# A two-layer graph network on 128 graphs: transposes of A and of score rows taken from TensorE to VectorE block transposes and GpSimd-issued DMAs

## The chip, the cores and the metric

The kernel runs on one core of a Trainium2 chip. Its engines work side by side, each through its own queue in order: TensorE (PE in the profile, with its weight loads as PEld) multiplies and can transpose; VectorE (DVE) and ScalarE (ACT) do the work element by element; GpSimd (POOL) and SyncE (SP) issue DMAs. Products land in PSUM, everything else lies in SBUF or in DRAM. The metric is the device time of one execution in microseconds (us); less is better.

## The reference

128 graphs of 128 nodes with 512 features; `adj` is a weighted 128x128 matrix for each. Cut to what matters (B = 128 graphs):

```python
# layer 0: graph attention, then K = 3 powers of the transition matrix
h = maximum(layernorm(x), 0)
Xw = h @ Wv + bv
sj, si = Xw @ aw[:512, 0], Xw @ aw[512:, 0]
e = leaky_relu(sj[:, None, :] + si[:, :, None] + ab[0], 0.2)     # score rows: sj runs along the row
alpha = adj * exp(e)
transition = alpha / (sum(alpha, -1, keepdims=True) + 1e-12)
H, Xk = 0, h
for k in range(3):
    H = H + Xk @ Wk[k] + bk[k]
    Xk = transition @ Xk
x = x + relu(H)
# layer 1
h2 = maximum(layernorm(x), 0)
q, k = split(h2 @ Wqk);  v = h2 @ Wv1
agg = adj @ (k * mask)
w = mask / sqrt(512) * sum(q * agg, -1)
x = x + softmax(w, axis=nodes)[:, :, None] * v
```

All data is fp32, and `mask` is given as an input.

## The kernel before

The kernel takes the graphs in pairs (G = 2, NP = 64 pairs) and is unrolled. Two algebraic turns matter for what follows. sj and si need no 512x512 product: two sums of h with fixed vectors u (`score_sums`) give them. And q times agg is h2 (Wq Wk^T) against A h2, so layer 1 multiplies h2 by two 512x512 matrices (`strassen1`) and A by h2 (`aggregate`). Both layers do their large products by a Strassen scheme with seven products P1 to P7, in the order 1, 6, 7, 5, 2, 3, 4. The framework puts the instructions of each engine in an order of its own, from the data they need and a model of their times, with the program's order as priority; it also sets the waits. A tile from a pool with `bufs=n` has n buffers in turn; a new tile waits until the oldest is no longer read.

Rows that have to be seen by all partitions are made by TensorE: `spread` transposes a column that is broadcast along the free axis.

```python
    def spread(dst, col):
        nc.tensor.transpose(dst, col.to_broadcast([P, P]), ident)
    # [...]
    def score_sums(p):
        h = H[p]
        s = S[p] = small.tile([P, G, 2], FP, name="s")
        for j in range(G):
            for a in range(2):
                junk = front.tile([P, D], FP, name="junk", bufs=1)
                nc.vector.scalar_tensor_tensor(junk, h[:, j, :], 1.0, u_bc[:, a, :], op0=OP.mult,
                                               op1=OP.mult, accum_out=s[:, j, a:a + 1])

    def by_blocks(h):
        hd = dram.tile([G, P, D], FP, name="hd")
        nc.sync.dma_start(hd.rearrange("g n d -> n g d"), h)
        hv = front.tile([P, G, Q, P], FP, name="hv")
        v = hd.rearrange("g (q b) (c i) -> c b (g q) i", b=S32, i=P)
        for c in range(DC):
            nc.sync.dma_start(hv[c * S32:(c + 1) * S32].rearrange("p g q i -> p (g q) i"), v[c])
        return hv

    def transposed(hv, dst):
        for j in range(G):
            nc.vector.transpose(dst[:, j].rearrange("p f (n b) -> p f n b", n=Q),
                                hv[:, j].rearrange("p n (f a) -> p f n a", f=Q))

    def attention(p):
        a, s = ag.pop(p), S.pop(p)
        pz = ps_t.tile([P, DC, P], FP, name="pt")
        for j in range(G):
            spread(pz[:, j, :], s[:, j, 0:1])
        z = front.tile([P, G, N], FP, name="z", bufs=1)
        for j in range(G):
            nc.vector.tensor_scalar(z[:, j, :], pz[:, j, :], s[:, j, 1:2], cz, op0=OP.add, op1=OP.add)
        nc.vector.scalar_tensor_tensor(z, z, 0.2, z, op0=OP.mult, op1=OP.max)
        ex = front.tile([P, G, N], FP, name="ex")
        nc.scalar.activation(ex, z, AF.Exp)
        d = small.tile([P, 2, G], FP, name="d")
        for j in range(G):
            nc.vector.scalar_tensor_tensor(ex[:, j, :], ex[:, j, :], 1.0, a[:, j, :], op0=OP.mult,
                                           op1=OP.mult, accum_out=d[:, 0, j:j + 1])
        nc.vector.tensor_scalar(d[:, 0], d[:, 0], 1e-12, None, op0=OP.add)
        nc.vector.reciprocal(d[:, 1], d[:, 0])
        t = T[p] = front.tile([P, G, N], FP, name="t")
        for j in range(G):
            nc.vector.tensor_scalar(t[:, j, :], ex[:, j, :], d[:, 1, j:j + 1], None, op0=OP.mult)
        pa = ps_t.tile([P, DC, P], FP, name="pt")
        for j in range(G):
            nc.tensor.transpose(pa[:, j, :], a[:, j, :], ident)
        AT[p] = front.tile([P, G, N], FP, name="aT", bufs=3)
        for j in range(G):
            b = p * G + j
            nc.scalar.activation(AT[p][:, j, :], pa[:, j, :], AF.Copy, scale=maskT[:, b:b + 1])

    def t_transposed(p):
        t, tt = T.pop(p), front.tile([P, G, 2, N], FP, name="tt")
        pt = ps_t.tile([P, DC, P], FP, name="pt")
        for j in range(G):
            nc.tensor.transpose(pt[:, j, :], t[:, j, :], ident)
        nc.scalar.copy(tt[:, :, 0, :], pt[:, :G, :])
        pt = ps_t.tile([P, DC, P], FP, name="pt")
        for j in range(G):
            nc.tensor.matmul(pt[:, j, :], t[:, j, :], tt[:, j, 0, :], start=True, stop=True)
        nc.scalar.copy(tt[:, :, 1, :], pt[:, :G, :])
        TT[p] = tt
```

`by_blocks` and `transposed` are a transpose without TensorE, and were there before: h goes to DRAM, is read back with its 32-row blocks exchanged, and VectorE transposes each 32x32 block. `ex` in `attention` is exp(e) times adj, `t` the transition matrix, and `AT` is A^T with the mask, from a transpose by TensorE.

```python
    def strassen0(p, steps):
        # [...]
        product(ba, 1, True)
        nc.vector.tensor_add(s[:, 0], a, hi)
        nc.vector.tensor_add(s[:, 1], a, lo)
        product(bb, 6, True)
        nc.vector.tensor_add(s[:, 2], b, s[:, 1])
        steps[0]()
        product(bc, 7, True)
        product(bb, 5, False)
        nc.vector.tensor_add(s[:, 3], b, s[:, 0])
        nc.vector.tensor_add(hb[:, 1, HD:], c, s[:, 3])
        steps[1]()
        product(ba, 2, False)
        nc.vector.tensor_add(hb[:, 0, :HD], a, lo)
        product(bb, 3, False)
        nc.vector.tensor_add(hb[:, 0, HD:], b, s[:, 0])
        product(bc, 4, False)
        nc.vector.tensor_add(hb[:, 1, :HD], c, s[:, 2])
        # [...]

    def strassen1(p):
        # [...]
        product(a, 1, True)
        nc.scalar.copy(s[:, 0], a)
        product(b, 6, True)
        nc.vector.tensor_add(s[:, 1], b, s[:, 0])
        product(c, 7, True)
        product(b, 5, False)
        nc.vector.tensor_add(s[:, 2], b, s[:, 0])
        nc.vector.tensor_add(o[1][1], c, s[:, 2])
        product(a, 2, False)
        nc.scalar.copy(o[0][0], a)
        product(b, 3, False)
        nc.vector.tensor_add(o[0][1], b, s[:, 0])
        product(c, 4, False)
        nc.vector.tensor_add(o[1][0], c, s[:, 1])
        return yv

    def aggregate(p, yv):
        h2, at = H2.pop(p), AT.pop(p)
        w = small.tile([P, 6, G], FP, name="w")
        for j in range(G):
            pa = ps_t.tile([P, D], FP, name="pt")
            nc.tensor.matmul(pa, at[:, j, :], h2[:, j, :], start=True, stop=True)
            junk = front.tile([P, D], FP, name="junk", bufs=1)
            b = p * G + j
            nc.vector.scalar_tensor_tensor(
                junk.rearrange("p (k d) -> p k d", k=2), pa.rearrange("p (k d) -> p k d", k=2),
                wscale[:, b:b + 1], yv[:, j, :, 0, :], op0=OP.mult, op1=OP.mult,
                accum_out=w[:, 0, j:j + 1])
        return w

    def finish(p, yv, w):
        pw = ps_t.tile([P, DC, P], FP, name="pt")
        for j in range(G):
            spread(pw[:, j, :], w[:, 0, j:j + 1])
        nc.vector.tensor_reduce(w[:, 1], pw[:, :G, :], AX.X, OP.max, negate=True)
        # [... exp of both rows with their sums, the weight of each node, x1 += weight * v ...]
        nc.sync.dma_start(out[p * G:(p + 1) * G].rearrange("b n d -> n b d"), x1)
```

The loop over pairs. In turn p, layer 0 of pair p runs with the attention of pair p + 1 between its products, then layer 1 of pair p - 1; `finish` (the softmax over the nodes) of an earlier pair runs inside the next layer 0.

```python
    for p in range(NP + 1):
        if p < NP:
            if p + 1 < NP:
                n = p + 1
                steps = (lambda: (begin(n), attention(n), end()), lambda: t_transposed(n))
            else:
                steps = (end, lambda: None)
            strassen0(p, steps)
            if p + 1 < NP:
                propagate(p + 1)
        # [...]
        if p < NP:
            H2[p] = norm_relu(X1[p], "h2", late["p"])
            hv2 = by_blocks(H2[p])
        if p > 0:
            yv = strassen1(p - 1)
            w = aggregate(p - 1, yv)
        if p + 1 < NP:
            prepare0(p + 1)
        if p > 0:
            ends.append((p - 1, yv, w))
        if p < NP:
            X2[p] = late["p"].tile([P, G, 2, HC, N], FP, name="x2")
            transposed(hv2, X2[p].rearrange("p j h c n -> p j (h c) n"))
            a = {(j, kh): X2[p][:, j, kh:kh + 1].rearrange("p k c n -> p k (c n)")
                 for j in range(G) for kh in range(2)}
            SX2[p] = left_sums(a, late["p"], "sx2", [1, HD])
        if p + 2 < NP:
            norm0(p + 2)
            score_sums(p + 2)
    end()
```

`late["p"]` is a pool with one buffer for each tile: h2, X2 and yv are single.

Of the kernel before, what the change touches and what calls it, by code (L numbers as in the profile page):

```python
# [8 lines left out]
FP = mybir.dt.float32  # L9
# [6 lines left out]
def kernel(  # L16
# [220 lines left out]

    H, HV, S, X, SX, AT, T, TT, X1, H2, X2, SX2 = ({} for _ in range(12))

# [7 lines left out]
    def score_sums(p):  # L248

        h = H[p]  # L250
        s = S[p] = small.tile([P, G, 2], FP, name="s")
        for j in range(G):
            for a in range(2):
                junk = front.tile([P, D], FP, name="junk", bufs=1)
                nc.vector.scalar_tensor_tensor(junk, h[:, j, :], 1.0, u_bc[:, a, :], op0=OP.mult,  # L255
                                               op1=OP.mult, accum_out=s[:, j, a:a + 1])

# [15 lines left out]

    def attention(p):

        a, s = ag.pop(p), S.pop(p)
        pz = ps_t.tile([P, DC, P], FP, name="pt")
        for j in range(G):
            spread(pz[:, j, :], s[:, j, 0:1])
        z = front.tile([P, G, N], FP, name="z", bufs=1)  # L280
        for j in range(G):
            nc.vector.tensor_scalar(z[:, j, :], pz[:, j, :], s[:, j, 1:2], cz, op0=OP.add, op1=OP.add)
        nc.vector.scalar_tensor_tensor(z, z, 0.2, z, op0=OP.mult, op1=OP.max)
        ex = front.tile([P, G, N], FP, name="ex")
        nc.scalar.activation(ex, z, AF.Exp)
        d = small.tile([P, 2, G], FP, name="d")
        for j in range(G):
            nc.vector.scalar_tensor_tensor(ex[:, j, :], ex[:, j, :], 1.0, a[:, j, :], op0=OP.mult,
                                           op1=OP.mult, accum_out=d[:, 0, j:j + 1])
        nc.vector.tensor_scalar(d[:, 0], d[:, 0], 1e-12, None, op0=OP.add)  # L290
        nc.vector.reciprocal(d[:, 1], d[:, 0])
        t = T[p] = front.tile([P, G, N], FP, name="t")
        for j in range(G):
            nc.vector.tensor_scalar(t[:, j, :], ex[:, j, :], d[:, 1, j:j + 1], None, op0=OP.mult)

        pa = ps_t.tile([P, DC, P], FP, name="pt")
        for j in range(G):
            nc.tensor.transpose(pa[:, j, :], a[:, j, :], ident)  # L298
        AT[p] = front.tile([P, G, N], FP, name="aT", bufs=3)
        for j in range(G):  # L300
            b = p * G + j
            nc.scalar.activation(AT[p][:, j, :], pa[:, j, :], AF.Copy, scale=maskT[:, b:b + 1])

    def t_transposed(p):

        t, tt = T.pop(p), front.tile([P, G, 2, N], FP, name="tt")
        pt = ps_t.tile([P, DC, P], FP, name="pt")
        for j in range(G):
            nc.tensor.transpose(pt[:, j, :], t[:, j, :], ident)  # L309
# [46 lines left out]
    def strassen0(p, steps):  # L356
# [53 lines left out]

    def aggregate(p, yv):

        h2, at = H2.pop(p), AT.pop(p)
        w = small.tile([P, 6, G], FP, name="w")
        for j in range(G):
            pa = ps_t.tile([P, D], FP, name="pt")
            nc.tensor.matmul(pa, at[:, j, :], h2[:, j, :], start=True, stop=True)  # L417
            junk = front.tile([P, D], FP, name="junk", bufs=1)
            b = p * G + j
            nc.vector.scalar_tensor_tensor(  # L420
                junk.rearrange("p (k d) -> p k d", k=2), pa.rearrange("p (k d) -> p k d", k=2),
                wscale[:, b:b + 1], yv[:, j, :, 0, :], op0=OP.mult, op1=OP.mult,
                accum_out=w[:, 0, j:j + 1])
        return w

    def finish(p, yv, w):

        pw = ps_t.tile([P, DC, P], FP, name="pt")
        for j in range(G):
            spread(pw[:, j, :], w[:, 0, j:j + 1])  # L430
        nc.vector.tensor_reduce(w[:, 1], pw[:, :G, :], AX.X, OP.max, negate=True)
        for j in range(G):
            ej = front.tile([P, N], FP, name="ej")
            nc.scalar.activation(ej, pw[:, j, :], AF.Exp, bias=w[:, 1, j:j + 1],
                                 accum_out=w[:, 2, j:j + 1])
        nc.vector.tensor_add(w[:, 3], w[:, 0], w[:, 1])
        nc.scalar.activation(w[:, 4], w[:, 3], AF.Exp)
# [100 lines left out]
```

## Time and profile before

| what | value |
|---|---|
| time, median of 3 runs | 2418.58 us (2418.56 to 2419.78) |
| span of the profiled execution | 2418.3 us |
| TensorE busy | 2378.8 us, 98% |
| VectorE busy | 1786.8 us, 74% |
| ScalarE busy | 650.5 us, 27% |
| GpSimd busy | 0.7 us |
| DMA queue of SyncE | 232624 packets, 216.65 MB, 30.5% of the 16 DMA engines' span |
| mean granted TensorE clock | 0.998 |

A line of a group reads: source line, engine, operation, output<-inputs, shapes, how often | busy us in total, mean ns of one | us that the engine sat idle just before them <- what ended it. In a timeline the two numbers ahead are the start and the length in us. A fp32 matmul shows as two instructions, a fp32 transpose as one. Matmuls follow each other in a pipeline, so that the distance of their starts is shorter than the length of one. A line of waits reads: engine and its work <- what it waited for: us in total, how often, longest.

### The profile page before, as it was taken

Reading aid. Unit: us, or ns where it says so; the run is one execution under the profiler, and the core shown is the slowest. Engines: PE = TensorE matmul, PEld = TensorE weight load, DVE = VectorE, ACT = ScalarE, POOL = GpSimd, SP = SyncE. Lnnn points to the kernel's source line nnn. Section 1 sums busy time; section 2 is a strip of 40 time slices with the busy share of each in tenths; the row PEclk is TensorE's granted clock in tenths of the full one; section 3 lists DMA queues with packets and bytes.
Section 4 is the critical chain, followed back from the end, with each engine's and each line's share of the span. In section 5 each row is a group of like instructions: output and inputs, shape, how many; then the busy total and the mean of one; then the engine's idle time right before and its main releaser. Section 6 shows DMA issues by size and latency. Waiting matters only on the chain.

```text
span 2418.3 us, 27245 instructions
## 1 busy us (share of the span) xinstructions
PE 2378.8 (98%) x9289; PEld 1694.5 (70%) x9289; DVE 1786.8 (74%) x4768; ACT 650.5 (27%) x1557; POOL 0.7 (0%) x6
## 2 busy tenths in 40 slices
PE   6999999999999999999999999999999999999997
PEld 4777677677676676776776776776766767767764
DVE  6777777777777777777777777777777777777764
ACT  3222222222222222223222222222222222232221
POOL 0000000000000000000000000000000000000000
PEclk9999999999999999999999999999999999999999
DMA  7233233233133233232332332332332332323311
GB/s 219 82 84 101 81 92 101 66 106 101 64 109 93 71 101 95 77 101 88 85 101 81 92 100 65 108 100 64 108 93 72 101 95 78 100 87 86 97 52 52
DMA packets 236986, 220.48 MB, mean 91 GB/s; under 512 B 14384, under 2 KB 170160, under 8 KB 236848
## 3 DMA queue, kind: packets, MB, share of 16 engines
q1 hardware_dynamic: 232624, 216.65, 30.5%
q10 hardware_dynamic: 4224, 2.10, 0.3%
q8 instruction: 73, 1.20, 0.2%
q14 instruction: 65, 0.53, 0.1%
HBM read 118.03 MB, written 100.66 MB: 90 GB/s over the span
## 4 chain that ended last, share of the span: by engine, by line
PE 96%; DVE 2%; DMA 1%; issue 0%; ACT 0%; SPq 0%; DVEq 0%; ACTq 0%
PE pm L346 79%; PE pt L325 9%; PE pt L417 4%; PE pt L97 1%; PE pt L313 1%; PE pt L298 1%; PE pt L309 1%; DMA bk_bc<-in_L_gnn_bk_dram 0%; DMA hd<-h 0%; DVE st L220 0%; DMA hv<-hd 0%; DMA w<-in_L_gnn_Wqk_dram 0%; DMA xg<-in_x_dram 0%; DVE x L271 0%; PE pm L208 0%
## 5 line engine op out<-in xcount | busy, mean ns | idle before, releaser
L346 PE MATMUL pm<-t,sx 128*128 128x256 f32 x2304 | 518.6, 380 | 1.4 <-DVE sx L333 1.4
L346 PEld LDWEIGHTS pm<-t,sx 128*128 128x128 f32 x2304 | 433.4, 190 | 57.4 <-DVE sx L333 2.0
L346 PE MATMUL pm<-b,x 128*128 128x256 f32 x1536 | 363.0, 380 | 0.0
L346 PE MATMUL pm<-f,sx 128*128 128x512 f32 x768 | 344.8, 598 | 0.3
L346 PEld LDWEIGHTS pm<-b,x 128*128 128x128 f32 x1536 | 282.6, 191 | 59.3 <-issue 29.6
L327 ACT COPY x<-pt 128x512 f32<-128x512 f32 x256 | 148.7, 581 | 500.6 <-PE pt L325 500.6
L346 PEld LDWEIGHTS pm<-f,sx 128*128 128x128 f32 x768 | 141.6, 191 | 193.7 <-issue 154.4
L346 PE MATMUL pm<-e,x 128*128 128x512 f32 x512 | 242.5, 596 | 6.5 <-DVE x L271 6.5
L325 PE MATMUL pt<-tt,h 128*128 128x256 f32 x1024 | 231.5, 379 | 0.0
L325 PEld LDWEIGHTS pt<-tt,h 128*128 128x128 f32 x1024 | 194.9, 190 | 26.2
L255 DVE SCALAR_TENSOR_TENSOR junk<-h,u_bc 128x512 f32<-128x512 f32 x256 | 176.4, 689 | 7.8 <-ACT h L235 0.9
L346 PE MATMUL pm<-b,sx 128*128 128x256 f32 x768 | 176.5, 379 | 0.0
L346 PE MATMUL pm<-t,x 128*128 128x256 f32 x768 | 176.2, 379 | 0.0
L235 ACT ACTIVATE h<-x,rs 128x512 f32<-128x512 f32 x128 | 97.2, 806 | 289.9 <-PE pt L417 277.1
L271 DVE STREAM_TRANSPOSE x<-hv 128x512 f32<-128x512 f32 x256 | 166.4, 688 | 6.6 <-DMA hv<-hd 5.7
L346 PEld LDWEIGHTS pm<-e,x 128*128 128x128 f32 x512 | 97.8, 191 | 102.8 <-issue 92.3
L346 PEld LDWEIGHTS pm<-t,x 128*128 128x128 f32 x768 | 146.2, 190 | 19.6
L346 PEld LDWEIGHTS pm<-b,sx 128*128 128x128 f32 x768 | 146.0, 190 | 19.5
L406 DVE TENSOR_TENSOR yv<-pm,s 128x512 f32<-128x512 f32 x64 | 44.3, 692 | 128.5 <-PE pm L346 128.5
L235 ACT ACTIVATE h<-xg,rs 128x512 f32<-128x512 f32 x128 | 97.2, 806 | 119.8 <-DVE rs L232 119.8
L417 PE MATMUL pt<-h,aT 128*128 128x512 f32 x256 | 120.5, 593 | 0.5 <-ACT h L235 0.5
L346 PE MATMUL pm<-e,sx 128*128 128x512 f32 x256 | 120.3, 592 | 0.0
(101 smaller groups left out, 2511.3 us busy)
## 6 DMA issues: line engine op xcount, KB each, us to landing
hd<-h SPq DMA_DIRECT2D x128, 512.0 KB, 3.1
hv<-hd SPq DMA_DIRECT2D x512, 128.0 KB, 3.3
xg<-in_x_dram SPq DMA_DIRECT2D x64, 512.0 KB, 3.6
out_dram<-x SPq DMA_DIRECT2D x64, 512.0 KB, 3.1
ag<-in_adj_dram SPq DMA_DIRECT2D x64, 128.0 KB, 3.0
w<-in_L_gnn_Wqk_dram ACTq DMA_DIRECT2D x8, 256.0 KB, 5.0
b<-in_L_gnn_Wk_dram SPq DMA_DIRECT2D x8, 256.0 KB, 3.4
wv_sb<-in_L_gnn_Wv_dram SPq DMA_DIRECT2D x4, 256.0 KB, 5.3
```

Source lines behind the costliest of these rows:

```text
L97: nc.tensor.transpose(dst, col.to_broadcast([P, P]), ident)
L235: nc.scalar.activation(h[:, j, :], src[:, j, :], AF.Relu, bias=rs[:, 1, j:j + 1], scale=rs[:, 0, j:j + 1])
L255: nc.vector.scalar_tensor_tensor(junk, h[:, j, :], 1.0, u_bc[:, a, :], op0=OP.mult, op1=OP.mult, accum_out=s[:, j, a:a + 1])
L271: nc.vector.transpose(dst[:, j].rearrange("p f (n b) -> p f n b", n=Q), hv[:, j].rearrange("p n (f a) -> p f n a", f=Q))
L298: nc.tensor.transpose(pa[:, j, :], a[:, j, :], ident)
L309: nc.tensor.transpose(pt[:, j, :], t[:, j, :], ident)
L313: nc.tensor.matmul(pt[:, j, :], t[:, j, :], tt[:, j, 0, :], start=True, stop=True)
L325: nc.tensor.matmul(pt[:, c].rearrange("p k n -> p (k n)"), h[:, j, at:at + P], tt[:, j].rearrange("p k n -> p (k n)"), start=True, stop=True)
L327: nc.scalar.copy(X[p][:, 1:3, j, kh].rearrange("p k c n -> p c k n"), pt)
L346: nc.tensor.matmul(bank[:, :r.shape[-1]], left[i][:, k, c * P:(c + 1) * P], r, start=(first and at == 0), stop=(at == len(chunks) - 1), sk ...
L406: nc.vector.tensor_add(o[0][1], b, s[:, 0])
L417: nc.tensor.matmul(pa, at[:, j, :], h2[:, j, :], start=True, stop=True)
```

## The change

Four things are done together.

1. A^T: A is loaded a second time by GpSimd's DMAs, with its 32x32 blocks exchanged, and one block transpose on VectorE then gives A^T. The two TensorE transposes of each pair and their PSUM tile go.
2. Score rows: the column sums are written to a 128x32 tile (cleared once), VectorE transposes its blocks, GpSimd writes the rows to DRAM with two DMAs and reads them back with one DMA broadcast to all partitions (`spread_pair`). It is used for layer 0's rows (pz) and for the rows of layer 1's softmax (pw); the first pair's pz and the last pair's pw still go by TensorE.
3. A h2 is computed between the products of layer 1 (after P7 and after P2) in place of after P4, and held in PSUM until P4 is through. The layer norm and the score sums of pair p + 2 are moved ahead, the sums to after P5.
4. z takes no tile of its own but the room of `s[:, 1]`, which is free once the sum after P6 of layer 0 is formed, so that it can't come before that sum in VectorE's queue. In the same way the negated peak of `finish` takes the room of `s[:, 3]`, free after the sums behind P5. ex is computed in place; t and tt go from two buffers to one.

What it is for: TensorE is rid of six transposes a pair, and waits for GpSimd's DMAs are kept from the head of VectorE's queue.

The diff, cut:

```diff
+        agb[p] = loads.tile([P, G, Q, S32], FP, name="agb", bufs=2)
+        v = adj[s].rearrange("g (q b) (c i) -> c b (g q) i", b=S32, i=S32)
+        for c in range(Q):
+            nc.gpsimd.dma_start(agb[p][c * S32:(c + 1) * S32].rearrange("p g q i -> p (g q) i"), v[c])
# [...]
+    cols = [const.tile([P, S32], FP, name=f"col{i}") for i in range(6)]
+    for t in cols:
+        nc.gpsimd.memset(t, 0.0)
# [...]
-        s = S[p] = small.tile([P, G, 2], FP, name="s")
+        s = S[p] = cols[p % 3]
         for j in range(G):
             for a in range(2):
                 junk = front.tile([P, D], FP, name="junk", bufs=1)
                 nc.vector.scalar_tensor_tensor(junk, h[:, j, :], 1.0, u_bc[:, a, :], op0=OP.mult,
-                                               op1=OP.mult, accum_out=s[:, j, a:a + 1])
+                                               op1=OP.mult, accum_out=s[:, a * G + j:a * G + j + 1])
+        PZ[p] = spread_pair(s, "pz", p > 0)
# [...]
-    def attention(p):
-        a, s = ag.pop(p), S.pop(p)
+    def spread_pair(col, name, by_dma):
+        if by_dma:
+            t = small.tile([P, S32], FP, name=f"{name}t", bufs=1)
+            nc.vector.transpose(t, col)
+            d = dram.tile([G, Q, S32], FP, name=f"{name}d")
+            for j in range(G):
+                nc.gpsimd.dma_start(d[j], t[j::S32])
+            dst = front.tile([P, G, N], FP, name=name, bufs=1)
+            nc.gpsimd.dma_start(dst.rearrange("p g n -> p (g n)"), bcast(d, 0, G * N))
+            return dst
         pz = ps_t.tile([P, DC, P], FP, name="pt")
         for j in range(G):
-            spread(pz[:, j, :], s[:, j, 0:1])
-        z = front.tile([P, G, N], FP, name="z", bufs=1)
-        for j in range(G):
-            nc.vector.tensor_scalar(z[:, j, :], pz[:, j, :], s[:, j, 1:2], cz, op0=OP.add, op1=OP.add)
+            spread(pz[:, j, :], col[:, j:j + 1])
+        return pz[:, :G]
+    def attention(p, room):
+        a, s, pz = ag.pop(p), S.pop(p), PZ.pop(p)
+        z = room.rearrange("p (g n) -> p g n", g=G)
+        for j in range(G):
+            nc.vector.tensor_scalar(z[:, j, :], pz[:, j, :], s[:, G + j:G + j + 1], cz, op0=OP.add, op1=OP.add)
         nc.vector.scalar_tensor_tensor(z, z, 0.2, z, op0=OP.mult, op1=OP.max)
-        ex = front.tile([P, G, N], FP, name="ex")
+        ex = z
# [...]
-        t = T[p] = front.tile([P, G, N], FP, name="t")
+        t = T[p] = front.tile([P, G, N], FP, name="t", bufs=1)
         for j in range(G):
             nc.vector.tensor_scalar(t[:, j, :], ex[:, j, :], d[:, 1, j:j + 1], None, op0=OP.mult)
-        pa = ps_t.tile([P, DC, P], FP, name="pt")
-        for j in range(G):
-            nc.tensor.transpose(pa[:, j, :], a[:, j, :], ident)
         AT[p] = front.tile([P, G, N], FP, name="aT", bufs=3)
+        nc.vector.transpose(AT[p].rearrange("p g n -> p (g n)"),
+                            agb.pop(p).rearrange("p g q i -> p (g q i)"))
         for j in range(G):
             b = p * G + j
-            nc.scalar.activation(AT[p][:, j, :], pa[:, j, :], AF.Copy, scale=maskT[:, b:b + 1])
+            nc.scalar.activation(AT[p][:, j, :], AT[p][:, j, :], AF.Copy, scale=maskT[:, b:b + 1])
# [...]
         product(bc, 7, True)
+        steps[1](s[:, 1])
         product(bb, 5, False)
         nc.vector.tensor_add(s[:, 3], b, s[:, 0])
         nc.vector.tensor_add(hb[:, 1, HD:], c, s[:, 3])
-        steps[1]()
+        steps[2]()
+        end(s[:, 3, :G])
         product(ba, 2, False)
         nc.vector.tensor_add(hb[:, 0, :HD], a, lo)
         product(bb, 3, False)
# [...]
-    def strassen1(p):
+    def strassen1(p, ahead):
# [...]
         product(c, 7, True)
+        agg = [aggregate(p, 0)]
         product(b, 5, False)
         nc.vector.tensor_add(s[:, 2], b, s[:, 0])
         nc.vector.tensor_add(o[1][1], c, s[:, 2])
+        if ahead < NP:
+            score_sums(ahead)
         product(a, 2, False)
         nc.scalar.copy(o[0][0], a)
+        agg.append(aggregate(p, 1))
+        H2.pop(p), AT.pop(p)
         product(b, 3, False)
         nc.vector.tensor_add(o[0][1], b, s[:, 0])
         product(c, 4, False)
         nc.vector.tensor_add(o[1][0], c, s[:, 1])
-        return yv
-    def aggregate(p, yv):
-        h2, at = H2.pop(p), AT.pop(p)
-        w = small.tile([P, 6, G], FP, name="w")
-        for j in range(G):
-            pa = ps_t.tile([P, D], FP, name="pt")
-            nc.tensor.matmul(pa, at[:, j, :], h2[:, j, :], start=True, stop=True)
+        return yv, scores(p, yv, agg)
# [...]
+    def aggregate(p, j):
+        pa = ps_t.tile([P, D], FP, name="pt")
+        nc.tensor.matmul(pa, AT[p][:, j, :], H2[p][:, j, :], start=True, stop=True)
+        return pa
+    def scores(p, yv, agg):
+        w = cols[3 + p % 3]
+        for j in range(G):
             junk = front.tile([P, D], FP, name="junk", bufs=1)
             b = p * G + j
             nc.vector.scalar_tensor_tensor(
-                junk.rearrange("p (k d) -> p k d", k=2), pa.rearrange("p (k d) -> p k d", k=2),
+                junk.rearrange("p (k d) -> p k d", k=2), agg[j].rearrange("p (k d) -> p k d", k=2),
                 wscale[:, b:b + 1], yv[:, j, :, 0, :], op0=OP.mult, op1=OP.mult,
-                accum_out=w[:, 0, j:j + 1])
+                accum_out=w[:, j:j + 1])
         return w
-    def finish(p, yv, w):
-        pw = ps_t.tile([P, DC, P], FP, name="pt")
-        for j in range(G):
-            spread(pw[:, j, :], w[:, 0, j:j + 1])
-        nc.vector.tensor_reduce(w[:, 1], pw[:, :G, :], AX.X, OP.max, negate=True)
+    def finish(peak, p, yv, ws, pw):
+        w = ws[:, :6 * G].rearrange("p (k g) -> p k g", g=G)
+        nc.vector.tensor_reduce(peak, pw, AX.X, OP.max, negate=True)
# [...]
-                steps = (lambda: (begin(n), attention(n), end()), lambda: t_transposed(n))
+                steps = (lambda: begin(n), lambda room: attention(n, room), lambda: t_transposed(n))
             else:
-                steps = (end, lambda: None)
+                steps = (lambda *_: None,) * 3
# [...]
+        if p + 2 < NP:
+            norm0(p + 2)
         if p > 0:
-            yv = strassen1(p - 1)
-            w = aggregate(p - 1, yv)
+            yv, w = strassen1(p - 1, p + 2)
+        elif p + 2 < NP:
+            score_sums(p + 2)
         if p + 1 < NP:
             prepare0(p + 1)
         if p > 0:
-            ends.append((p - 1, yv, w))
+            ends.append((p - 1, yv, w, spread_pair(w, "pw", p < NP)))
# [...]
-        if p + 2 < NP:
-            norm0(p + 2)
-            score_sums(p + 2)
```

More of the change, by code (lines that the diff above doesn't have):

```diff
@@ L64, in bcast @@
         return bass.AP(tensor=ap.tensor, offset=ap.offset + offset, ap=[[0, P], [1, n]])
-    xg, ag = {}, {}
+    xg, ag, agb = {}, {}, {}
     def load(p):
@@ L237, in norm_relu @@
         return h
-    H, HV, S, X, SX, AT, T, TT, X1, H2, X2, SX2 = ({} for _ in range(12))
+    cols = [const.tile([P, S32], FP, name=f"col{i}") for i in range(6)]
+    for t in cols:
+        nc.gpsimd.memset(t, 0.0)
+    H, HV, S, PZ, X, SX, AT, T, TT, X1, H2, X2, SX2 = ({} for _ in range(13))
     def norm0(p):
@@ L291, in attention @@
         nc.vector.reciprocal(d[:, 1], d[:, 0])
-        t = T[p] = front.tile([P, G, N], FP, name="t")
+        t = T[p] = front.tile([P, G, N], FP, name="t", bufs=1)
         for j in range(G):
             nc.vector.tensor_scalar(t[:, j, :], ex[:, j, :], d[:, 1, j:j + 1], None, op0=OP.mult)
-        pa = ps_t.tile([P, DC, P], FP, name="pt")
-        for j in range(G):
-            nc.tensor.transpose(pa[:, j, :], a[:, j, :], ident)
         AT[p] = front.tile([P, G, N], FP, name="aT", bufs=3)
+        nc.vector.transpose(AT[p].rearrange("p g n -> p (g n)"),
+                            agb.pop(p).rearrange("p g q i -> p (g q i)"))
         for j in range(G):
             b = p * G + j
-            nc.scalar.activation(AT[p][:, j, :], pa[:, j, :], AF.Copy, scale=maskT[:, b:b + 1])
+            nc.scalar.activation(AT[p][:, j, :], AT[p][:, j, :], AF.Copy, scale=maskT[:, b:b + 1])
     def t_transposed(p):
-        t, tt = T.pop(p), front.tile([P, G, 2, N], FP, name="tt")
+        t, tt = T.pop(p), front.tile([P, G, 2, N], FP, name="tt", bufs=1)
         pt = ps_t.tile([P, DC, P], FP, name="pt")
@@ L420, in aggregate @@
             nc.vector.scalar_tensor_tensor(
-                junk.rearrange("p (k d) -> p k d", k=2), pa.rearrange("p (k d) -> p k d", k=2),
+                junk.rearrange("p (k d) -> p k d", k=2), agg[j].rearrange("p (k d) -> p k d", k=2),
                 wscale[:, b:b + 1], yv[:, j, :, 0, :], op0=OP.mult, op1=OP.mult,
-                accum_out=w[:, 0, j:j + 1])
+                accum_out=w[:, j:j + 1])
         return w
-    def finish(p, yv, w):
-        pw = ps_t.tile([P, DC, P], FP, name="pt")
-        for j in range(G):
-            spread(pw[:, j, :], w[:, 0, j:j + 1])
-        nc.vector.tensor_reduce(w[:, 1], pw[:, :G, :], AX.X, OP.max, negate=True)
+    def finish(peak, p, yv, ws, pw):
+        w = ws[:, :6 * G].rearrange("p (k g) -> p k g", g=G)
+        nc.vector.tensor_reduce(peak, pw, AX.X, OP.max, negate=True)
         for j in range(G):
             ej = front.tile([P, N], FP, name="ej")
-            nc.scalar.activation(ej, pw[:, j, :], AF.Exp, bias=w[:, 1, j:j + 1],
+            nc.scalar.activation(ej, pw[:, j, :], AF.Exp, bias=peak[:, j:j + 1],
                                  accum_out=w[:, 2, j:j + 1])
-        nc.vector.tensor_add(w[:, 3], w[:, 0], w[:, 1])
+        nc.vector.tensor_add(w[:, 3], w[:, 0], peak)
         nc.scalar.activation(w[:, 4], w[:, 3], AF.Exp)
@@ L453 @@
     score_sums(0)
-    attention(0)
+    attention(0, front.tile([P, D], FP, name="junk", bufs=1)[:, :G * N])
     uctx.close()
@@ L470, with end @@
     ends = []
-    def end():
+    def end(peak=None):
         while ends:
-            finish(*ends.pop())
+            finish(small.tile([P, G], FP, name="peak") if peak is None else peak, *ends.pop())
     for p in range(NP + 1):
```

## The prediction, made before the change was run

> **What bounds the kernel now.** I read the busy times first, then the same by stage, then TensorE's groups by shape, then the timeline of one turn of the steady state, and last the DMA list and the end of the run. The page's first part:
>
> ```profile
> PE 2378.8 (98%) x9289; PEld 1694.5 (70%) x9289; DVE 1786.8 (74%) x4768; ACT 650.5 (27%) x1557; POOL 0.7 (0%) x6
> ```
>
> TensorE (PE) is busy for 98% of the span; GpSimd (POOL) does nothing. Two successive turns of the loop over pairs, cut at the first product of layer 1:
>
> ```profile
> core 0: us, PE busy (x) PEld busy (x) DVE busy (x) ACT busy (x) POOL busy (x), PEclk, DMA share, GB/s
> 1200.77:1237.47 36.70, 36.70 (x146) 26.26 (x145) 27.59 (x75) 10.01 (x24) 0.00 (x0) 1.00 0.28 90
> 1237.47:1274.17 36.70, 36.70 (x146) 26.25 (x145) 27.59 (x75) 10.00 (x24) 0.00 (x0) 1.00 0.31 89
> ```
>
> A turn lasts 36.70 us and PE works through all of it, at full clock. VectorE (DVE) has 36.70 - 27.59 = 9.1 us to spare, the DMA engines 70%. So in the steady state the turn is PE's instruction stream and nothing else, and an instruction taken from it shortens the turn by the room it takes up in the stream, if no new wait appears. The three kinds that the change takes out, in TensorE's groups by shape:
>
> ```profile
> L97 PE MATMUL pt<-ident,s 128*128 128x128 f32 x128 | 25.2, 276 | 2.0 <-DVE junk L255 1.9
> L97 PE MATMUL pt<-ident,w 128*128 128x128 f32 x128 | 24.9, 274 | 1.3 <-DVE junk L420 1.3
> L298 PE MATMUL pt<-ident,ag 128*128 128x128 f32 x128 | 24.7, 275 | 0.0
> ```
>
> Their mean of 275 ns is not their price: matmuls overlap in the pipeline. The price is the distance of starts, which the timeline of the turn gives:
>
> ```profile
> 1219.74 0.38 PE L97 MATMUL pt<-ident,s 128*128 128x128 f32 x2
> 1219.95 0.38 PE L298 MATMUL pt<-ident,ag 128*128 128x128 f32 x2
> 1220.17 0.38 PE L97 MATMUL pt<-ident,w 128*128 128x128 f32 x2
> 1220.39 5.35 PE L346 MATMUL pm<-t,sx 128*128 128x256 f32 x24
> 1225.57 0.38 PE L309 MATMUL pt<-ident,t 128*128 128x128 f32 x2
> ```
>
> Six transposes stand between P6 and P7 of layer 0 and hold the stream for 1220.39 - 1219.74 = 0.65 us, 0.108 us each. The transposes of t at 1225.57 stay.
>
> **What the Trainium skill says.** Three places. (1) "VectorE: DVE Perf Modes", section The three transpose paths: VectorE transposes only within 32x32 blocks, SBUF to SBUF. The trace agrees in kind: L271 already does this, 128x512 in 688 ns. This is why A needs a load that exchanges blocks before the block transpose can finish A^T. (2) "DMA: Bandwidth & Descriptors", section Anatomy of one DMA — SWDGE (gpsimd) path: a DMA from GpSimd has a fixed cost of about 2.0 us, most of it waiting for the write to be confirmed. No GpSimd DMA is in this trace; those of SyncE land after 3.0 to 3.6 us in the median (2.2 the shortest for the 128 KB loads of A), so I use 3 to 4 us a hop, not 2.0. (3) "SBUF — State Buffer", section Who interferes with whom: a VectorE tensor_scalar between SBUF operands can hold the port over which GpSimd writes descriptors. No run here shows it; such work in the trace is L294 with 280 ns, twice a turn, and z will join it, so about 1 us a turn.
>
> **The change, part by part.**
>
> *A^T.* Two transposes a pair leave PE: 64 x 2 x 0.108 = 13.8 us of the stream. Added: four GpSimd DMAs a pair in pieces of 128 bytes (1024 of them, 128 KB) and one VectorE block transpose of 128x256; from L271's 688 ns for 512 columns and the 425 ns of other 256-wide operations, 0.42 us. Its load is issued two turns ahead, so its latency is beside the path. ScalarE still scales by the mask, now from SBUF in place of PSUM (363 ns before): ScalarE is 27% busy, no effect.
>
> *Score rows z.* 63 pairs (all but the first) no longer use PE: 63 x 2 x 0.108 = 13.6 us. Instead: block transpose of a 128x32 column tile, 0.2 us; two small DMAs to DRAM; one that broadcasts them to 128 partitions. Two hops that depend on each other, and these lie near the path.
>
> *Softmax rows of layer 1 (w).* Again 63 pairs, 13.6 us, with the same two hops. finish is tied behind a sum after P5, at about 1226 on the old clock; w is done at 1216. About 10 us for 0.2 + two hops of 3 to 4 us: hidden.
>
> *A h2 between the products.* The same two matmuls move, nothing is saved on PE. But h2 has one buffer, and these matmuls are its last readers. ScalarE waits for them:
>
> ```profile
> ACT h L235 <- PE pt L417: 277.1, 61, 4.6
> ```
>
> That is 4.6 us a turn; it falls to about 1 us, since the last reader now comes before P3 and P4 (two products of 1.72 us = 3.4 us). Inside the loop that is no gain, since PE never waits there for h2. It counts once, at the end.
>
> *The end.* The longest wait of PE in the whole run:
>
> ```profile
> PE pt L97 <- DVE r L227: 13.1, 1, 13.1
> PE pm L346 <- DVE x L271: 6.5, 1, 6.5
> ```
>
> The 13.1 us are the start, unchanged. The 6.5 us are the last pair: h2 is written at 2384.84 (free at last), goes through DRAM, and PE's last layer 1 begins at 2394.32. With h2 free 3.4 us earlier that start moves by up to 3.4 us; I count 2.5, as the last A h2, which filled part of this gap, may now stand in the stream.
>
> *Score sums ahead.* They move from behind layer 1 (1215.99 to 1219.1) into VectorE's idle time inside it (2.02 us before L406, 1.02 before L408). This is what gives z's two hops their time.
>
> **Sum.** PE's stream loses 13.8 + 13.6 + 13.6 = 41.0 us. Of the first two turns (0.43 us each, where PE waits on sx right after anyway) and the last w, lying in the gap at the end, I take off 1.0: 40.0. The end gives 2.5. GpSimd's DMAs ahead of ident and the extra VectorE work during the start take back perhaps 0.5 us. 2418.6 - 40.0 - 2.5 + 0.5 = 2376.6. I allow about 2 us for small new waits in 62 turns: **2379 us**, a gain of 1.6%. A turn should last 36.05 us.
>
> **Rivals.**
>
> *A. z's row comes late and PE waits at t's transposes.* On the old clock: h is written at 1208.3; four score sums of 0.69 + 0.08 us between L402 and L408 end at about 1212.9; transpose and semaphores, 1213.2; two issues on GpSimd and a landing, 1217 to 1218; issue and broadcast, 1220.5 to 1222. z can begin at 1220.4 (behind P6's sum). From z to t the trace needs 3.9 us (L282 at 1220.28 to the end of L294 at 1224.20), but finish's operations stand between; without them about 3 us. The transposes of t come after P5, at 1220.39 + 5.18 - 0.65 = 1224.9. So z may begin as late as about 1221.9: a slack between +1.4 and 0 us. Every microsecond beyond it costs PE up to 1 us a turn; a hop of 4.5 us in place of 3.5 makes two more, 62 x (2 - 0.7) = 80 us: then about 2460. For it: no GpSimd DMA has been measured here. Against: the order of instructions is fixed beforehand by a schedule that knows the DMAs; P2 can stand before t's transposes, which propagate only needs 8 us later; and the tie behind P6's sum shows that the queue was thought of. A mild form, 0.3 us a turn, makes 2397.
>
> *B. VectorE's queue blocks.* VectorE works in order. If z or finish stands at its head waiting for a DMA, L373 (the sum after P5) waits behind it, and P3 needs that bank. L373 has one product, 2.6 us, before PE feels it. So only a delay of over 2.6 us beyond the planned time hurts; the same DMAs as in A decide it. Time as in A.
>
> *C. GpSimd or the DMA engines become slow.* Ten GpSimd DMAs a turn, and 1024 + 16 + 256 more packets beside some 3600 (232624 packets / 64). At 51 ns a packet (30.5% x 16 x 2418 us / 232624) the additions are 1296 x 51 / 16 = 4.1 us of each engine in 36: from 30% to 42%. hd and hv may land some tenths later; X2 is ready 7 us before its use (sums end at 1229.8, P1 at 1237.47). It costs nothing unless GpSimd's issue takes more than 3.6 us each.
>
> *D. VectorE becomes the bound.* 27.6 + 0.42 + 2 x 0.2 - 2 x 0.12 (z from SBUF, 280 in place of 402 ns) = 28.2 of 36.05 us. No.
>
> **Range and chances.** Without any new wait the floor is 2375, and a larger share of the end or a warmer clock there might give 3 more: 2372. Over 2% would need 2370.2 or less, beyond what PE is rid of: 6%. Rival A or B in a mild form (up to 0.6 us a turn) leads to 2380 to 2415, with perhaps three chances in ten; slower by 2% (2467) needs 1.4 us of new wait in every turn: 6%. So 88% within 2%. Range 2371 to 2412.
>
> **What would show it.** Right: no transposes of s, w or ag but for the first and last pairs; a turn of 36.05 us with PE busy in all of it; L420's and finish's waits off PE; ScalarE's wait for A h2 down to about 1 us; the end's gap shorter by 2 to 3.5 us. Wrong: PE idle before t's transposes or before P3, put down to z or to a DMA of pz; a turn longer than 36.4 us; GpSimd DMAs landing after more than 4.5 us; a longer start because ident comes late. If PE's stream is free of gaps and the turn is still above 36.05, then my price of 0.108 us a transpose is wrong.

## The result and the profile after

The changed kernel takes 2396.8 us (median; 2395.8 to 2398.4), the kernel before, beside it, 2418.8 us. The ratio is 0.9909, with a 95% interval of 0.9892 to 0.9926: 22 us or 0.9% faster, and 18 us slower than the predicted 2379. The profiled executions last 2418.3 us before and 2394.7 us after; the times below are theirs.

The page's first part, and the chain of work that ended last by engine:

```profile
PE 2338.7 (98%) x8909; PEld 1656.8 (69%) x8909; DVE 1830.6 (76%) x4958; ACT 635.4 (27%) x1557; POOL 369.7 (15%) x646
...
PE 86%; DVE 6%; DMA 4%; issue 2%; ACT 1%; POOL 0%; DVEq 0%; SPq 0%; POOLq 0%; ACTq 0%
```

TensorE has 380 matmuls fewer (9289 - 8909) and is still busy for 98%. GpSimd now issues DMAs. DMAs hold 4% of the chain; that share, some 90 us, isn't time lost: TensorE works beside most of it. The two turns in the middle of the run that answer to those shown of before:

```profile
core 0: us, PE busy (x) PEld busy (x) DVE busy (x) ACT busy (x) POOL busy (x), PEclk, DMA share, GB/s
1192.60:1228.58 35.98, 35.98 (x139) 25.70 (x138) 28.22 (x78) 9.76 (x25) 5.84 (x10) 1.00 0.38 104
1228.58:1264.57 35.99, 35.99 (x140) 25.70 (x139) 28.23 (x78) 9.78 (x25) 5.82 (x10) 1.00 0.40 103
```

A steady turn fell from 36.70 to 35.98 us, with TensorE busy in all of it. So the middle of the loop does what was planned, and a little more. TensorE's waits for others (total, times, longest) show where it doesn't:

```profile
PE pt L101 <- DVE r L231: 16.2, 1, 16.2
PE pm L367 <- DVE x L279: 13.7, 2, 10.4
...
PE pm L367 <- DVE s L421: 4.8, 7, 1.4
...
PE pt L330 <- DVE t L316: 1.4, 1, 1.4
```

The first wait was 13.1 us and is the start; the second had 6.5 as its longest, and 10.4 is the end. The third is seven turns in the middle.

**The balance.** I cut both spans at the first products of layer 1. Up to the second layer 1: 136.1 us before, 143.9 after, +7.8. The 61 turns from there to the last boundary: 2234.8 and 2201.6, -33.2. From there to the end: 47.4 and 49.2, +1.8. The sum is -23.6, the whole difference of the spans. In the middle, 61 x 0.715 = 43.6 us would have been won, but eleven turns (8, 9, 18, 28, 38 to 40, 48 and 58 to 60, counted from the first layer 1) last 36.2 to 38.0 us and give back 10.8. (Two turns of 37.05 us before, and a last turn that saves only 0.22 us, make the small rest.)

### The profile page after: what moved, and what is told of

The parts are those of the page before. It is cut to its first block, busy times and chain, and to the rows that moved or that the text cites. A ratio compares the mean times of both kernels' runs of the same rounds, so it can differ in the third digit from the quotient of the medians. Undisturbed runs are those within 1.5% of the kernel's fastest.

```text
span 2394.7 us, 27824 instructions
## 1 busy us (share of the span) xinstructions
PE 2338.7 (98%) x8909; PEld 1656.8 (69%) x8909; DVE 1830.6 (76%) x4958; ACT 635.4 (27%) x1557; POOL 369.7 (15%) x646
## 3 DMA queue, kind: packets, MB, share of 16 engines
q0 software_dynamic: 22304, 25.09, 5.9%
## 4 chain that ended last, share of the span: by engine, by line
PE 86%; DVE 6%; DMA 4%; issue 2%; ACT 1%; POOL 0%; DVEq 0%; SPq 0%; POOLq 0%; ACTq 0%
PE pm L367 72%; PE pt L346 8%; PE pt L442 4%; DMA pwd<-pwt 2%; DMA pw<-pwd 1%; PE pt L334 1%; DVE st L224 1%; PE pm L212 1%; PE pt L330 1%; DVE x L279 1%; DVE x L407 0%; DVE sx L354 0%; DVE sx L353 0%; DVE sx L355 0%; DMA pzd<-pzt 0%
## 5 line engine op out<-in xcount | busy, mean ns | idle before, releaser
L367 PE MATMUL pm<-t,sx 128*128 128x256 f32 x2304 | 507.9, 379 | 1.9 <-DVE sx L354 1.9
L367 PE MATMUL pm<-f,sx 128*128 128x512 f32 x768 | 352.9, 595 | 4.8 <-DVE s L421 4.8
L290 POOL DMA_DIRECT2D pzd<-pzt x126 | 69.9, 556 | 1443.4 <-DVE pzt L287 1443.2
L367 PE MATMUL pm<-e,x 128*128 128x512 f32 x512 | 242.9, 597 | 13.7 <-DVE x L279 13.7
L279 DVE STREAM_TRANSPOSE x<-hv 128x512 f32<-128x512 f32 x256 | 166.3, 687 | 7.5 <-DMA hv<-hd 5.6
L307 ACT ACTIVATE s<-s 128x256 f32<-128x256 f32 x63 | 26.2, 416 | 522.8 <-DVE s L305 522.8
L77 POOL DMA_DIRECT2D agb<-in_adj_dram x256 | 152.9, 602 | 18.1 <-DVE aT L319 7.4
L442 PE MATMUL pt<-h,aT 128*128 128x512 f32 x256 | 130.6, 592 | 0.0
```

The source lines that it names most:

```text
L77: nc.gpsimd.dma_start(agb[p][c * S32:(c + 1) * S32].rearrange("p g q i -> p (g q) i"), v[c])
L290: nc.gpsimd.dma_start(d[j], t[j::S32])
L367: nc.tensor.matmul(bank[:, :r.shape[-1]], left[i][:, k, c * P:(c + 1) * P], r, start=(first and at == 0), stop=(at == len(chunks) - 1), sk ...
L442: nc.tensor.matmul(pa, AT[p][:, j, :], H2[p][:, j, :], start=True, stop=True)
```

## The experiments

Ratios are to the kernel before, run beside each. Where the text says "pairs 0 to 2 by TensorE", z's rows and A^T are made as in the kernel before for these pairs; the loads of A in blocks are left out for them. All kernels compute the whole reference; e13 only adds copies that nobody reads.

**e1: A h2 between the products, alone.** The kernel before, with this one part of the change.

```
         product(c, 7, True)
+        agg = [a_h2(p, 0)]
         product(b, 5, False)
 ...
         nc.scalar.copy(o[0][0], a)
+        agg.append(a_h2(p, 1))
```

> The kernel before, with A h2 alone moved between layer 1's products. Theory 1 (the second matmul after P7 gives VectorE time for the sum that P5's bank waits for, 0.06 us a turn, and h2 is free 3.4 us earlier at the end): turn 36.64 us in place of 36.70, end shorter by 2 to 3.4 us, in all 2411 to 2413 us. Rival (moving it changes nothing on TensorE): 2418 us, turn 36.70.

Measured: 2412.7 us, ratio 0.9969 (0.9954 to 0.9984). The turn is 36.64 us, 0.06 shorter, and the last wait for x falls from 6.5 to 4.0 us. 61 x 0.06 = 3.7 of the turns and 2.5 of the end make 6.2 of the 7.4 us between the two profiled spans. So this part is worth something inside the loop too. In the kernel before, TensorE's weight loads waited in 63 turns for a sum; this line is gone:

```profile
PEld pm L346 <- DVE s L398: 38.8, 63, 1.0
```

**e2: A^T alone.** The kernel before, with A^T by GpSimd's loads and a block transpose; t and tt have one buffer here too.

```
-            nc.tensor.transpose(pa[:, j, :], a[:, j, :], ident)
+        nc.vector.transpose(AT[p]..., agb.pop(p)...)
```

> The kernel before, with A^T alone by GpSimd loads and block transposes. Theory 1 (two transposes of 0.108 us go, and only the start loses: the first block transpose waits at the head of VectorE's queue for its load): turn 36.48 us, start later by about 3 us, no long turns, about 2408 us. Rival 2 (the GpSimd DMAs as such slow hd and hv and cause long turns): several turns over 36.9 us, 2412 us or more.

Measured: 2408.1 us, ratio 0.9950 (0.9935 to 0.9965). The turn is 36.48 us, 0.22 shorter, which is two transposes of 0.108 us; the first layer 1 starts 1.2 us later. One turn of 36.83 us is the only long one. A^T is as cheap as planned.

**e3 and e4: the start by TensorE; w's rows by TensorE.** Two kernels, each the changed one with one edit.

```
e3  PZ[p] = spread_pair(s, "pz", p > 2)        # was p > 0; pair 0 loads no agb
e4  ends.append((p - 1, yv, w, None))          # and in finish:
    pw = spread_pair(ws, "pw", False)
```

> The changed kernel, but pairs 0 to 2 take their score rows, and pair 0 its A^T, from TensorE as before. Theory 1 (the start loses about 8 us to waits for GpSimd's DMAs at the head of VectorE's queue): the second layer 1 begins at 136 to 138 us in place of 143.9, in all 2389 to 2391 us; long turns stay. Rival (the start is longer because of the different order and the DMA load): no more than 2 us come back, 2395 us.

> The changed kernel, but layer 1's rows w go by TensorE again. Theory 1 (a late pw row at the head of VectorE's queue makes the turns longer than 36 us, 10.8 us in all, and 3 us at the end): turn 36.20 us, hardly a turn over 36.3, end 3 us shorter; the two returned transposes cost 62 x 0.22 = 13.6 us, so 2396 us, the same. Rival 2 (the long turns come from GpSimd's DMAs in general): the long turns stay, and 2407 us or more.

Measured: e3 2393.9 us, ratio 0.9888 (0.9872 to 0.9905); e4 2392.0 us, ratio 0.9883 (0.9868 to 0.9898). In e3 the second layer 1 starts at 139.3 instead of 143.9 (136 to 138 was expected), but the last wait for x is 11.7 us and the long turns stay (10.4 us), so less than the expected gain is left. In e4 a turn takes 36.20 us, 0.22 more as two transposes are back, yet no turn is long (0.14 us in all) and the last wait for x is 3.9 us. Putting w's rows back on TensorE beats the changed kernel: a part of the change that saves 0.22 us in each turn loses more than it saves.

**e5: z's rows by TensorE, w's by DMA.** The complement of e4.

```
-        PZ[p] = spread_pair(s, "pz", p > 0)
+        pz = spread_pair(s, "pz", False)      # in attention
```

> The mirror of the run before: the changed kernel with layer 0's rows z by TensorE, w's rows by GpSimd's DMAs. Theory 1 (the pw row is the cause of the long turns): long turns stay; turn 36.20 us between them. If the late pw every tenth turn comes with a count of GpSimd's own instructions (10 DMAs a turn), its distance grows to about 14 turns with 7 DMAs a turn. The start comes about 5 us earlier than in the changed kernel (no wait for pz). 2400 to 2406 us. Rival (z's rows, not w's, lengthen the turns): no long turns, 2392 us.

Measured: 2405.0 us, ratio 0.9941 (0.9926 to 0.9956). The time lies in the expected range, but by another way. After the third turn only one is longer than 36.38 us (36.57), so w's rows by DMA alone don't make long turns: with seven DMAs a turn w's row is issued 4.8 us behind its column in the median (6.8 in the changed kernel), no pause falls ahead of it, and finish doesn't wait for it in the loop. But a turn takes 36.38 us, not 36.20: z's spread stands behind P7 now, and VectorE waits 2.4 us a turn for it. I can't account for all of the 0.18.

**e6: finish later.** If finish blocks VectorE's queue while it waits for w's row, it should stand behind P3's sum.

```
         steps[2]()
-        end(s[:, 3, :G])
 ...
         nc.vector.tensor_add(hb[:, 0, HD:], b, s[:, 0])
+        end(s[:, 0, :G])
```

> The changed kernel with finish tied behind the sum after P3 in place of those after P5, so that its first operation stands about 4 us later in VectorE's queue. Theory 1 (a pw row up to 2.7 us late blocks VectorE's queue there): no wait for pw in the loop, turn 35.98 us throughout, 10 us less than the changed kernel, 2386 us. Rival (the long turns come from the DMA load of that turn, the wait of VectorE is a sign only): long turns stay, 2396 us.

Measured: 2476.0 us, ratio 1.0236 (1.0221 to 1.0252). The expectation failed. TensorE's and VectorE's waits, and the landings of z's two hops (median us), of e6:

```profile
PE pt L330 <- DVE t L316: 67.1, 55, 3.2
```

```profile
DVE s L304 <- DMA pz<-pzd: 177.7, 62, 4.9
```

```profile
pz<-pzd POOLq DMA_DIRECT2D x63, 128.0 KB, 4.9
pzd<-pzt POOLq DMA_DIRECT2D x126, 0.5 KB, 3.5
```

The wait for w's row is gone from the loop (24.0 us in 29 turns in the changed kernel), as the theory said. But finish's operations now stand among the norms, the score sums behind these end 1.8 us later, and z's column is issued 12.1 us after the start of a turn instead of 10.0. From its issue to that of the row takes 5.2 us instead of 2.7, and z begins at 22.4 us instead of 19.6. This small DMA lands after 3.5 us here and after 1.6 us in the changed kernel. That it meets the transfers of h, issued about then, fits but was argued only. In all but a few turns TensorE waits at t. That is rival A of the prediction, brought about by a column that is issued 2.1 us later.

**e8 and e9: more than one edit.** e8 is e4 with pairs 0 to 2 by TensorE. e9 is e6 with the same start, and with the last two of w's rows by TensorE.

```
e8  e4's edit; PZ[p] = spread_pair(s, "pz", p > 2); A^T of p <= 2 by nc.tensor.transpose
e9  e6's edit; the same start; spread_pair(w, "pw", p < NP - 1)
```

> w's rows by TensorE throughout, and z's rows and A^T of the first three pairs too (no GpSimd load before that of pair 3). Theory 1 (the start loses to waits on GpSimd's DMAs and to their load beside that of x): first transposes at 13.1 us and second layer 1 at 136 us as in the kernel before, 7 us less than with w's rows alone by TensorE, 2385 us. Rival (the start is long for its order): 2390 us or more.

> All remedies with the rows of w still by GpSimd: finish behind the sum after P3, first three pairs by TensorE, last two pw rows by TensorE. Theory 1: turn 35.98 us, start as before (second layer 1 at 136 us), end 3 to 4 us shorter than in the changed kernel: 2396.8 - 10.8 - 7 - 3.5 = 2375 us. Rival (remedies interfere, the later finish delays other work of VectorE): 2385 us or more.

Measured: e8 2388.6 us, ratio 0.9873 (0.9858 to 0.9887), 4 us above what was expected; the start's gain adds to that of e4. e9 2470.6 us, ratio 1.0217 (1.0200 to 1.0234): a miss by 96 us, for the reason of e6.

**e10, e11, e12: A's loads by SyncE; the start and the end by TensorE; both.**

```
e10  nc.sync.dma_start(agb[p]..., v[c])                 # was nc.gpsimd
e11  e8's start; spread_pair(w, "pw", p < NP - 1)       # was p < NP; other rows of w by DMA
e12  e10's edit and e11's
```

> The changed kernel, with the four loads for A^T issued by SyncE instead of GpSimd: six GpSimd DMAs a turn instead of ten[...]. Theory 1 (the late issue of w's row in every tenth turn belongs to GpSimd's DMA queue: something comes due after about a hundred of its DMAs): the long turns come every 16 or 17 turns or hardly at all, their excess over the steady turn falls from 10.8 us to 6.5 or less, and the time from 2396.8 to 2386 to 2393. Theory 2 (it is something of the loop or of time, which doesn't count GpSimd's DMAs): long turns every tenth turn as before, 2396 to 2397. Theory 3 (SyncE's queue, which also holds h's two hops, becomes late): the steady turn grows above 36.0 us with waits on x, more than 2397.

> The changed kernel, with z's rows and A^T of pairs 0 to 2 and w's rows of the last two pairs by TensorE. Theory (start and end each lost a few us to DMAs waiting at the head of VectorE's queue, apart from the long turns): the second layer 1 starts at 138.5 instead of 143.9 (-5.4), the last wait of TensorE for x falls from 10.4 to about 4 to 6 us (-5), the long turns stay: 2396.8 - 10 = 2387. Rival (what e8 gained came from the middle alone, where w's row by TensorE ended the long turns): the end stays, 2392 to 2394.

> Both edits in one. If theory 1 of the first run and the theory of the second hold, the gains add, as they lie in different stretches: 2396.8 - 4 to -11 - 10 = 2376 to 2383, the best of all. If the long turns stay: 2387, as the second run.

Measured: e10 2387.1 us, ratio 0.9871 (0.9854 to 0.9887); e11 2377.2 us, ratio 0.9829 (0.9814 to 0.9844); **e12 2373.8 us, ratio 0.9811 (0.9796 to 0.9825), the fastest of all**, 2 us below its expected range, and it still uses all of the change's parts in the steady turns. e12's waits of TensorE, and a turn of it:

```profile
PE pt L103 <- DVE r L233: 13.7, 1, 13.7
PE pt L103 <- DVE junk L127: 5.2, 6, 4.0
PE pm L375 <- DVE x L281: 4.4, 1, 4.4
```

```profile
1186.90:1222.90 36.00, 36.00 (x139) 25.58 (x138) 26.64 (x74) 10.05 (x24) 3.36 (x6) 1.00 0.38 103
```

In e10 one turn of 37.1 us is left. Against the changed kernel's profile, e11 is 5.1 us shorter up to the second layer 1, 10.0 in the 61 turns and 5.8 behind them: together 20.9, the whole difference of the spans. So start and end behave as expected, but the middle was better than I had expected: the long turns are gone but for one of 36.4 us, although e11 still issues all ten DMAs a turn from GpSimd. That left the theory behind e10 (a pause tied to GpSimd's queue) alive, but not its reason: the pause is still there in e11, at another place.

**e13: three more DMAs at the start.** To move that place and nothing else.

```
+    extra = dram.tile([3, P], FP, name="extra", bufs=1)
+    for k in range(3):
+        nc.gpsimd.dma_start(extra[k], adj[0, k])
```

> The changed kernel with three more small GpSimd DMAs (0.5 KB each, DRAM to DRAM, nothing uses them) at the start, and nothing else. Theory (GpSimd's issue pauses by 2 to 3 us at a fixed spacing along its own stream of instructions, and the long turns come only because that place falls on the issue of w's row, the last of the turn's ten): the pause comes three DMAs earlier in the turn, on the second pair of loads for A^T, as in e11, where nobody waits for it; the long turns 8, 18, 28, 38, 48, 58 go, and their excess falls from 10.8 us to under 2: 2386 to 2388. Rival (the pause goes with something of the loop, or e10 and e11 lost it by their other edits): long turns every tenth turn as before, 2396 to 2398.

Measured: 2400.5 us, ratio 0.9924 (0.9908 to 0.9941). The long turns stay at 8, 18, 28, 38, 48 and 58: the theory fell. GpSimd's timeline in turn 17 of e13 shows the pause where it was, ahead of w's row, which is issued 3.0 us after its column has landed. (The profile names a copy by ScalarE that ended 0.4 us before; the pause is as long as in the turns where it names none.)

```profile
700.73 1.16 POOL L293 DMA_DIRECT2D pwd<-pwt  x2 [1.50 <-DVE pwt L290]
710.11 0.59 POOL L295 DMA_DIRECT2D pw<-pwd  x1 [8.21 <-ACT tt L334]
```

## Why the prediction came out as it did

It was right that the kernel gets faster by less than 2%, and the time lies in its range. The median is missed by 18 us, and the steps are uneven. Its "mild form" of rival A, 0.3 us a turn, even names 2397; that this is the measured number is chance, as TensorE waits for t only once, 1.4 us.

**The price of a transpose held.** Six of them were to give 0.65 us a turn. e2 gives 0.22 for two, e4 takes 0.22 back for two. The turn is 0.72 shorter, not 0.65.

**"Inside the loop that is no gain" failed, to the good.** ScalarE's wait for the last reader of h2 fell from 277.1 us, 4.6 at a time, to this:

```profile
ACT h L239 <- PE pt L442: 17.3, 63, 0.3
```

But the two products also stand where a weight load used to wait for a sum, and e1 shows 0.06 us a turn for it. With the transposes that makes 36.70 - 0.65 - 0.06 = 35.99. The stream's 40.0 became 43.6.

**Rival A and B's timing held in the steady turn, by luck as much as by reasoning.** VectorE and GpSimd in one turn:

```profile
1202.57 1.11 POOL L290 DMA_DIRECT2D pzd<-pzt  x2 [22.84 <-DVE pzt L287]
...
1205.29 0.58 POOL L292 DMA_DIRECT2D pz<-pzd  x1 [0.23 <-issue]
...
1208.56 1.17 POOL L290 DMA_DIRECT2D pwd<-pwt  x2 [1.52 <-DVE pwt L287]
1214.68 0.59 POOL L292 DMA_DIRECT2D pw<-pwd  x1 [4.95 <-DMA pwd<-pwt]
```

```profile
1211.71 0.42 DVE L390 TENSOR_TENSOR s<-pm,s 128x256 f32<-128x256 f32 x1 [1.83 <-PE pm L367]
1212.17 0.60 DVE L304 TENSOR_SCALAR s<-pz,col,cz 128x128 f32<-128x128 f32 x2
...
1218.90 0.41 DVE L461 TENSOR_REDUCE s<-pw 128x2 f32<-128x256 f32 x1
```

z (L304) has no wait of its own and stands right behind P6's sum (L390). Its row was issued at 1205.29 and lands 5.3 us later in the median, at about 1210.6: 1.6 us of margin. I had worked with 3 to 4 us a hop. The small first hop takes 1.6 us in the median for z, but 5.5 us for w with the same bytes. "DMA: Bandwidth & Descriptors" of the Trainium skill, section Anatomy of one DMA — SWDGE (gpsimd) path, gives about 2.0 us of fixed cost; the first number lies a little below it, the second far above. A single figure for a hop was the weak place of my sum; z was saved by its score sums standing 2 us earlier than they do in e6. There is some slack behind it, too: in turn 21 of e10 z's row is issued 2.9 us late, z waits 1.1 us for it, and the turn still takes 35.98 us.

**Rivals C and D stayed off the path.** VectorE's 28.2 us a turn are as forecast. GpSimd's queue moved 22304 packets, some 350 a turn and not 1296, yet h's second hop landed 2.0 us later in the median, not some tenths; the steady turn didn't feel it.

**"About 2 us for small new waits in 62 turns" failed: it was 10.8.** In those turns the step that breaks is "About 10 us for 0.2 + two hops of 3 to 4 us: hidden", on w. The chain in turns 27 and 28, first GpSimd, then VectorE and TensorE's weight load:

```profile
1063.69 1.16 POOL L290 DMA_DIRECT2D pwd<-pwt  x2 [1.33 <-DVE pwt L287]
1072.40 0.59 POOL L292 DMA_DIRECT2D pw<-pwd  x1 [7.55 <-issue]
```

```profile
1075.75 0.42 DVE L461 TENSOR_REDUCE s<-pw 128x2 f32<-128x256 f32 x1 [1.63 <-DMA pw<-pwd]
...
1089.51 0.69 DVE L421 TENSOR_TENSOR s<-pm,s 128x512 f32<-128x512 f32 x1
```

```profile
1090.25 0.30 PEld L367 LDWEIGHTS pm<-f,sx 128*128 128x128 f32 x2 [1.19 <-DVE s L421]
```

w's row is issued 8.7 us behind its column instead of the 6.1 of the turn above. As a rule it follows the column's landing after 0.6 us, but in turns 7, 17, 27, 37, 47 and 57 after 2.7 to 3.0. (Ahead of turns 9, 39, 40, 59 and 60 the landing itself is late, 7.5 to 8.1 us; why right behind the pause isn't shown.) finish stands at the head of VectorE's queue and waits 1.63 us for it. Everything behind it shifts: norms, X2's sums, then L421, the sum after P6 of the next layer 1. P5's weights wait for L421's bank for 1.19 us, where 0.24 is the usual spacing. In turns 8, 9, 18, 28, 38, 39, 48 and 58, TensorE loses its time at this same product (0.2 to 1.7 us), and 0.3 us more at P3. So rival B's way was right, its place wrong: I looked for the sum after P5 in the same turn (2.6 us of slack), and the delay comes out 14 us later, in a part with less slack. e4, e5, e11 and e12 all lose these turns, with the late issue ahead of w's row gone or fallen elsewhere.

**The start, "+0.5", was +7.8.** Up to the second layer 0 it is 2.6 us (77.4 instead of 74.9), and from there to the second layer 1 another 5.2 (66.5 instead of 61.3).

The 2.6 come with the loads of A in blocks. One line offers itself as the cause, as pair 0's norm stands behind this transpose and doesn't need it; but in e3, which leaves pair 0's transpose to TensorE, pair 1's x comes hardly earlier, and the second layer 0 begins at 78.0. The changed kernel, e3, and e12:

```profile
11.23 0.45 DVE L319 STREAM_TRANSPOSE aT<-agb 128x256 f32<-128x256 f32 x1 [4.32 <-DMA agb<-in_adj_dram]
13.53 1.29 DVE L224 BATCH_NORM_STATS2 st<-xg 128x6 f32<-128x512 f32 x2 [1.02 <-DMA xg<-in_x_dram]
```

```profile
12.87 1.29 DVE L226 BATCH_NORM_STATS2 st<-xg 128x6 f32<-128x512 f32 x2 [5.01 <-DMA xg<-in_x_dram]
```

```profile
11.03 1.29 DVE L226 BATCH_NORM_STATS2 st<-xg 128x6 f32<-128x512 f32 x2 [2.57 <-DMA xg<-in_x_dram]
```

Pair 1's x lands at 10.5 us in the kernel before and in e1, at 11.0 in e12, whose first block load is issued at 56.7 us, and at 12.5 to 13.7 wherever GpSimd issues such loads in the first 6 us, in e11 too. That the two get in each other's way in the DMA engines fits, but wasn't measured by itself.

The 5.2 are z's rows. In the first turns the score sums aren't ahead yet, z waits 4.2 us for its row, and X2's transposes, on which TensorE waits, stand behind z; one turn later z waits 3.2 us, and TensorE the 1.4 us for t:

```profile
96.47 0.60 DVE L304 TENSOR_SCALAR s<-pz,col,cz 128x128 f32<-128x128 f32 x2 [4.21 <-DMA pz<-pzd]
```

```profile
100.26 2.39 PE L367 MATMUL pm<-e,x 128*128 128x512 f32 x4 [3.29 <-DVE x L279]
```

Where TensorE makes these rows (e3, e5, e8, e9, e11, e12) this stretch takes 60.6 to 61.8 us, where DMAs make them (e4, e6, e10, e13) 64.5 to 66.4. I had taken off 0.43 us a turn for these turns and never drawn their timeline. e11 takes 5.1 us of the start back, e12 9.0.

**The end, "-2.5", was +1.8.** The same figure once more, in the last turn:

```profile
2367.68 0.42 DVE L461 TENSOR_REDUCE peak<-pw 128x2 f32<-128x256 f32 x1 [6.48 <-DMA pw<-pwd]
...
2370.84 0.70 DVE L279 STREAM_TRANSPOSE x<-hv 128x512 f32<-128x512 f32 x1
```

```profile
2371.60 2.08 PE L367 MATMUL pm<-e,x 128*128 128x512 f32 x2 [10.45 <-DVE x L279]
```

The move of A h2 does bring its 2.5 us (e1). But with no other work in the queue, finish waits 6.5 us for w's row, and the last pair's X2 (L279) stands behind it. e11 makes that row on TensorE, idle there anyway, and the wait is 4.3 us.

So of the miss, 7.3 us are the start, 8.8 the long turns and 4.3 the end, against 3.6 to the good in the steady turns: 16.8, within a us of the 17.8 measured.

**What stays open: why w's row is issued late in one turn of ten.** The profile puts such pauses down to "issue". With A's loads on SyncE, the same pause of some 3 us comes in turns 21 and 41, once ahead of z's row and once ahead of w's column; the second, in e10:

```profile
1559.08 0.57 POOL L292 DMA_DIRECT2D pz<-pzd  x1 [1.87 <-DMA pzd<-pzt]
1564.49 1.13 POOL L290 DMA_DIRECT2D pwd<-pwt  x2 [4.84 <-issue]
```

In e11 it falls between two loads of A, in turns 20, 30, 40 and 50, where nobody waits; turn 30:

```profile
1159.87 0.60 POOL L79 DMA_DIRECT2D agb<-in_adj_dram  x1
1162.66 0.58 POOL L79 DMA_DIRECT2D agb<-in_adj_dram  x1 [2.19 <-issue]
```

So the pause belongs to GpSimd's own stream, comes about twice as often with ten DMAs a turn as with six, and moves when A's loads are taken out ahead of it. It is not a fixed count of DMAs (100 between pauses in one, 121 in the other, and e13), nor of packets (3520 and some 4500). That e11 and e12 are nearly free of long turns (at most 36.5 us) is shown; that they are so by design is not: a small edit may bring them back.

## What to carry to other kernels

When a small value's way goes through DRAM to save a bottleneck engine's instruction, the reader that waits for it stands at the head of an in-order queue; so follow what stands behind it into the next turn, and draw the first and the last turn by themselves, where the slack of the steady state is missing. Keep the old way where the bottleneck engine has to wait anyway (first and last pairs here), hold back loads that nobody needs yet while the first data come in, and put DMAs whose time isn't critical on another queue than those that are: together that doubled the gain of this change, from 22 to 46 us.

## What had not been expected of the hardware

- The same DMA of 0.5 KB from GpSimd lands after 1.6 us in one place of the turn and 5.5 us in another (medians), after 3.5 us if it is issued 2.1 us later (e6).
- GpSimd's issue of one DMA takes 0.56 to 0.60 us of the engine, and every hundred or so (100 with ten DMAs a turn, 121 with six) it pauses for 2 to 3 us.
- hd and hv, the two hops of h on SyncE's queue, land after 3.9 and 5.3 us (3.1 and 3.3 before) with the additional transfers beside them.
